# A graph diffusion with a routed feed-forward layer on one core: the last source tile stacked in the first step too, built blocks moved by 128 bytes, and early adds on VectorE

## The chip, the core and the metric

The program runs on one core of one Trainium2 chip. Its engines appear in the profile as PE (TensorE, matrix products into PSUM; PEld are its weight loads), DVE (VectorE), ACT (ScalarE), POOL (GpSimd) and SP (SyncE, here an issuer of DMA transfers). The metric is device time in microseconds (us); lower is better. "Profiled execution" means the one execution that the hardware profiler recorded; its own time is longer than its span by what lies around the first and the last instruction.

## The reference, cut to what matters

There are 3125 nodes with 256 features and 103,125 directed edges (50,000 in both directions, plus loops). The values at the edges' sources are summed at their destinations, divided by the degree, and this is repeated six times, each time divided by the step's number:

```python
def _spmm(h, src, dst, inv_deg):
    msg = h[src]
    agg = jax.ops.segment_sum(msg, dst, num_segments=h.shape[0])
    return agg * inv_deg[:, None]
...
out = h
term = h
for i in range(1, k + 1):                 # k = 6, gamma = 0
    term = (_spmm(term, src, dst, inv_deg) + gamma * term) / float(i)
    out = out + term
```

Around it: `h` is silu of a projection of the normalised input; the result is projected once more and added to the input. Then a router picks two of eight experts for each node, and their weighted outputs are added.

## The kernel before

Nodes are cut into 25 tiles of 128 rows (`NT = 25`, `P = 128`); the last has 53 rows only (`LAST`), less than half (`HP = 64`). The output projection is applied ahead of the diffusion, so that the terms have 256 columns (`D`) all the way.

**Terms in two parts.** A term is kept as two fp32r numbers, the rounded value and the rest, side by side: `t0` and `t1` are `[128, 25, 512]`. `split` (L350) makes both: a cast into the first 256 columns and a subtraction into the last 256. `t0` holds the terms of even steps, `t1` those of odd ones. Both begin at an address that is 480 modulo 512 bytes in each partition.

**Blocks.** For each destination tile j there is a block `blk` of 128 x 3200 numbers: for each source tile i a 128 x 128 piece that counts the edges from a source row to a destination row. `build_tile(j)` (L628) builds it in two halves: VectorE makes one-hot matrices (`left`, L638, and five `right`, L647), TensorE multiplies them in 40 small bf16 products (`pa`, L658), and ScalarE copies four results into the block (L662). The buffers of a half (pool `hot`) and the block's own (pool `blocks`, at 352 modulo 512 bytes) are double. At the end SP stores the block to DRAM (`adj[j]`). The last source tile has its real rows in the lower 64 partitions; in DRAM both halves of its piece hold the same numbers:

```python
full = (NT - 1) * P
nc.sync.dma_start(adj[j][:, :full], blk[:, :full].bitcast(F32))          # L666
for p in (0, HP):
    nc.sync.dma_start(adj[j][p:p + HP, full:], blk[:HP, full:].bitcast(F32))   # L668
```

**First step.** For each j, block j + 1 is built first, and then 25 products `pd` (L703), each 128 x 512, add up block j times `t0`. `finish` (L671) follows: ScalarE scales the columns of the rests (`low`, L675), VectorE forms `term` (L677) and writes both parts of it to `t1`. Engines run their instructions in the order in which a scheduler put them when the program was built.

**Steps two to six** (L1006 on). The block is loaded from `adj[j]` (L1008; pool `blocks2`, four buffers, at 480 modulo 512 bytes), in order on SP's queue, where the stores of the first step stand too. Here the last source tile is *stacked*: since only 64 of its partitions are needed, the upper 64 hold the term's parts crosswise (L681 to L683), and as both halves of the block's piece are equal, one 256-column product adds value and rest at once. It is multiplied second to last. `finish` adds the new term to the sum `acc` (L687) from the second step on.

**Early adds.** The projected input and the first step's term are added to `acc` later, in the second and the third step, by `add_late` (L689): three adds for a tile in the second step (with the bias), two in the third, on GpSimd. They read a tile of the buffer that `finish` writes anew in the same round.

**After the sixth step** come the lists of the router, the experts (L954, L963) and the weighted sums; the change does not touch them.

Of the kernel before, what the change touches and what calls it, by code (L numbers as in the profile page):

```python
# [10 lines left out]
F32 = mybir.dt.float32  # L11
# [9 lines left out]
P = 128  # L21
# [2 lines left out]
NT = 25  # L24
LAST = N - (NT - 1) * P
HP = P // 2
NE = 103125
NCH = (NE + P - 1) // P
G = 12
# [237 lines left out]
def tile_gnn_then_moe(  # L267
# [82 lines left out]
    def split(dst, v):  # L350
        nc.vector.tensor_copy(dst[:, :D], v)
        nc.vector.tensor_sub(dst[:, D:], v, dst[:, :D].bitcast(F32))

    lane = keys.tile([P, NH, CK, HALF], F16, name="lane")
# [180 lines left out]
                                  pk.rearrange("p k (h w) -> p k h w", w=HALF))  # L537
    before.close()
    hot = build.enter_context(tc.tile_pool(name="hot", bufs=2, reuse_waits="tile"))
    blocks = build.enter_context(tc.tile_pool(name="blocks", bufs=2, reuse_waits="tile"))  # L540
    ps_a = build.enter_context(tc.tile_pool(name="ps_a", bufs=2, space=bass.MemoryType.PSUM,
                                            reuse_waits="tile"))
# [33 lines left out]
    for t in range(0, NT, 2):  # L576
        n = min(2, NT - t)
        xt = proj.tile([P, 2, 2 * P], F32, name="xt")
        nc.scalar.copy(xt[:, :, :n * P], pt[:, :, :n * P])
        if t + 2 < NT:  # L580
            pt = normed(t + 2)
        ph = ps_o.tile([P, 2, 2 * P], F32, name="ph")
        ht = proj.tile([P, 2, 2 * P], F32, name="ht")
        for c in range(2):
            for k in range(2):
                nc.tensor.matmul(ph[:, c, :n * P], w_in_sb[:, k, c * P:(c + 1) * P], xt[:, k, :n * P],
                                 start=(k == 0), stop=(k == 1))
            nc.scalar.activation(ht[:, c, :n * P], ph[:, c, :n * P], AF.Silu,
                                 bias=b_in_pm[:, c:c + 1], scale=1.0)
        pm = ps_o.tile([P, 2, D], F32, name="pm")  # L590
        for q in range(n):
            for c in range(2):
                nc.tensor.matmul(pm[:, q, :], ht[:, c, q * P:(q + 1) * P], w_out_sb[:, c, :],
                                 start=(c == 0), stop=(c == 1))
        nc.vector.tensor_copy(t0[:, t:t + n, :D], pm[:, :n, :])
        nc.vector.tensor_sub(t0[:, t:t + n, D:], pm[:, :n, :], t0[:, t:t + n, :D].bitcast(F32))
    intro.close()
    ps_1 = build.enter_context(tc.tile_pool(name="ps_1", bufs=2, space=bass.MemoryType.PSUM,
                                            reuse_waits="tile"))
# [28 lines left out]
    def build_tile(j):  # L628
        blk = blocks.tile([P, NT * P], F32R, name="blk")
        by_dst = blk.rearrange("p (i q) -> p q i", q=P)  # L630
        for h in (2 * j, 2 * j + 1):
            if h * HALF * W >= N:
                half = blk.rearrange("p (i q) -> p i q", q=P)
                nc.vector.tensor_copy(half[:, :, HP:], half[:, :, :HP].bitcast(F32))
                continue
            left = hot.tile([P, CK, HALF // 2, P, 2], BF16, name="left")
            nl = CK * HALF // 2
            nc.vector.tensor_tensor(  # L638
                left.rearrange("p k a l u -> p (k a) l u"),
                steps[:, None, :P, :].to_broadcast([P, nl, P, 2]),  # L640
                lane[:, h, :, :].rearrange("p k (a u) -> p (k a) u", u=2)[:, :, None, :]
                .to_broadcast([P, nl, P, 2]), op=ALU.is_equal)
            right = []
            for k, (a, b) in enumerate(SPAN):
                m = (b - a) * NT
                r = hot.tile([P, HALF // 2, m, 2], BF16, name=f"right{k}")
                nc.vector.tensor_tensor(  # L647
                    r, steps[:, None, :m, :].to_broadcast([P, HALF // 2, m, 2]),
                    place[:, h, k, :].rearrange("p (a u) -> p a u", u=2)[:, :, None, :]
                    .to_broadcast([P, HALF // 2, m, 2]), op=ALU.is_equal)  # L650
                right.append(r)
            for a in range(HALF // 2):

                n = 2 * h + a
                pa = (ps_b if j > 1 and n % 3 == 2 else ps_a).tile([P, 2, 512], F32, name="pa")
                for u in range(2):
                    for k, (lo, hi) in enumerate(SPAN):
                        nc.tensor.matmul(pa[:, u, lo * NT:hi * NT], left[:, k, a, :, u],  # L658
                                         right[k][:, a, :, u], start=(k == 0), stop=(k == CK - 1),
                                         skip_group_check=True)  # L660
                q = ((h % 2) * HALF + 2 * a) * W
                nc.scalar.copy(  # L662
                    by_dst[:, q:q + 2 * W, :].rearrange("p (u q) i -> p u q i", u=2),
                    pa[:, :, :W * NT].rearrange("p u (q i) -> p u q i", i=NT))
        full = (NT - 1) * P
        nc.sync.dma_start(adj[j][:, :full], blk[:, :full].bitcast(F32))  # L666
        for p in (0, HP):
            nc.sync.dma_start(adj[j][p:p + HP, full:], blk[:HP, full:].bitcast(F32))  # L668
        return blk

    def finish(j, pd, step, new):  # L671
# [2 lines left out]
        low = work.tile([P, D], F32, name="low")  # L674
        nc.scalar.activation(low, pd[:, D:], AF.Copy, scale=inv)  # L675
        term = work.tile([P, D], F32, name="term")
        nc.vector.scalar_tensor_tensor(term, pd[:, :D], inv, low, op0=ALU.mult, op1=ALU.add)  # L677
        if new is not None and j < NT - 1:
            split(new[:, j, :], term)
        elif new is not None:  # L680
            nc.vector.tensor_copy(new[:HP, j, :D], term[:HP])  # L681
            nc.vector.tensor_copy(new[HP:, j, D:], term[HP:])
            nc.vector.tensor_sub(new[HP:, j, :D], term[HP:], new[HP:, j, D:].bitcast(F32))  # L683
            if step == 1:
                nc.vector.tensor_sub(new[:HP, j, D:], term[:HP], new[:HP, j, :D].bitcast(F32))
        if step > 1:
            nc.vector.tensor_add(acc[:, j, :], acc[:, j, :], term)  # L687

    def add_late(j, t, bias):  # L689

        term = early.tile([P, D], F32, name="early")
        part = t[:, j, :].bitcast(F32)
        nc.gpsimd.tensor_add(term, part[:, :D], part[:, D:])  # L693
        if bias:
            nc.gpsimd.tensor_add(term, term, b_out_sb)
        nc.gpsimd.tensor_add(acc[:, j, :], acc[:, j, :], term)

    blk = build_tile(0)
    for j in range(NT):
        ahead = build_tile(j + 1) if j + 1 < NT else None  # L700
        pd = ps_1.tile([P, 2 * D], F32, name="pd")
        for i in range(NT):
            nc.tensor.matmul(pd, blk[:, i * P:(i + 1) * P], t0[:, i, :],  # L703
                             start=(i == 0), stop=(i == NT - 1))
        finish(j, pd, 1, t1)
        if 8 <= j < 8 + len(tests):
            check_spans(j - 8)
        elif j == 8 + len(tests):
# [291 lines left out]
    for step in range(2, STEPS + 1):  # L1000
# [5 lines left out]
        for j in range(NT):  # L1006
            blk = blocks.tile([P, NT * P], F32R, name="blk")
            nc.sync.dma_start(blk.bitcast(F32), adj[j])  # L1008
            if step < 4:
                add_late(j, new, step == 2)  # L1010
            pd = ps_d.tile([P, 2 * D], F32, name="pd")
            for i in [*range(NT - 2), NT - 1, NT - 2]:
                n = D if i == NT - 1 else 2 * D
                nc.tensor.matmul(pd[:, :n], blk[:, i * P:(i + 1) * P], old[:, i, :n],  # L1014
                                 start=(i == 0), stop=(i == NT - 2), skip_group_check=True)
            finish(j, pd, step, new if step < STEPS else None)
            if step == STEPS:
                route(j)
    lists_end()
# [83 lines left out]
```

## Time and profile before

| What | us |
|---|---|
| median of four runs (1339.10 to 1341.39) | 1340.15 |
| profiled execution, its own time | 1344.07 |
| its span, first to last instruction | 1342.30 |
| first product of the first step (L703) begins | 96.32 |
| last product of the first step begins | 327.3 |
| second step's first product (L1014) begins | 330.81 |
| last product of the sixth step begins | 1057.4 |
| VectorE busy, whole span | 582.0 |
| GpSimd busy, whole span | 208.6 |

The rows of the last two lines are sums over the span. The others are places in it: the first step takes from 96 to 328, the five following steps from 331 to 1058, the experts and sums the rest. A matmul's row in the trace begins when it starts; its end is modelled, and the next matmul starts before it. So the distance between two starts is what a product costs in a row of products, not the length in the row.

### The profile page before, as it was taken

The page shows a single profiled execution, that of the slowest core. Times are in us where ns is not written, and L with a number is a line of the kernel's source. Part 1 is how long each engine was busy: PE and PEld are TensorE (multiplying, and loading weights), DVE is VectorE, ACT ScalarE, POOL GpSimd, SP SyncE. Part 2 cuts the span into 40 slices and gives each one's busy share as a digit, 9 for nine tenths or more (in the row PEclk, how much of TensorE's full clock was granted, in tenths as well). Part 3 has the DMA queues.
Part 4 walks back from the last instruction along what each step waited for, and adds up shares of the span by engine and source line. Part 5 has one row for each costly group of instructions (what it writes and reads, how often), then busy time and mean ns, then how long its engine had stood idle before and what let it go on. Part 6 is the DMA issues. An engine that isn't in the chain of part 4 may idle for free. (4 is left out here: it accounts for less than half of the span.)

```text
span 1342.3 us, 16667 instructions
## 1 busy us (share of the span) xinstructions
PE 1233.9 (92%) x6181; PEld 1017.6 (76%) x6181; DVE 582.0 (43%) x1436; ACT 347.2 (26%) x534; POOL 208.6 (16%) x264
## 2 busy tenths in 40 slices
PE   4999999999999999999999999999999559999940
PEld 2778888887888888888888888887777448888830
DVE  6769999994432222222222222245555412222116
ACT  5656667673000000000000000012222212222210
POOL 2000000007942200000000000001233222222210
PEclk9999999999999999999999999999999869999985
DMA  6014343436888888888888888887888277677728
GB/s 196 1 73 173 148 196 147 197 147 266 326 293 295 294 296 294 293 294 294 294 293 296 293 295 294 296 300 257 283 283 282 73 218 222 215 249 228 236 87 270
DMA packets 86246, 318.47 MB, mean 237 GB/s; under 512 B 12254, under 2 KB 56237, under 8 KB 66953
## 3 DMA queue, kind: packets, MB, share of 16 engines
q1 hardware_dynamic: 74550, 297.14, 62.5%
q0 software_dynamic: 5280, 14.54, 3.1%
q10 hardware_dynamic: 6322, 5.60, 1.3%
q8 instruction: 52, 0.85, 0.2%
q14 instruction: 42, 0.34, 0.1%
HBM read 256.44 MB, written 60.81 MB: 236 GB/s over the span
## 5 line engine op out<-in xcount | busy, mean ns | idle before, releaser
L1014 PE MATMUL pd<-t,blk 128*128 128x512 f32 (+1 forms) x3125 | 714.4, 388 | 3.1 <-DMA blk<-adj 3.1
L1014 PEld LDWEIGHTS pd<-t,blk 128*128 128x128 f32 x3125 | 576.2, 189 | 120.8 <-issue 3.5
L677 DVE SCALAR_TENSOR_TENSOR term<-pd,inv_deg,low 128x256 f32<-128x256 f32 x150 | 72.4, 483 | 454.5 <-ACT low L675 454.4
L675 ACT ACTIVATE low<-pd,inv_deg 128x256 f32<-128x256 f32 x150 | 71.1, 474 | 650.5 <-PE pd L1014 578.5
L703 PE MATMUL pd<-t,blk 128*128 128x512 f32 x625 | 151.1, 398 | 0.0
L662 ACT CAST blk<-pa 128x800 fp32r<-128x800 f32 x98 | 146.7, 1652 | 12.2 <-PE pa L658 12.2
L703 PEld LDWEIGHTS pd<-t,blk 128*128 128x128 f32 x625 | 115.9, 188 | 25.3
L647 DVE TENSOR_TENSOR right<-steps,place 128x800 bf16<-128x800 f16 (+3 forms) x245 | 127.9, 577 | 3.3 <-PE pa L658 3.3
L954 PE MATMUL ph<-xt,w_sb 128*128 128x256 f32 x432 | 100.6, 387 | 2.4 <-DMA w_sb<-in_w_dram 1.3
L658 PE MATMUL pa<-right,left 128*128 128x200 bf16 (+3 forms) x980 | 98.9, 254 | 0.9 <-ACT blk L662 0.7
L963 PE MATMUL py<-w_sb,ht 128*128 128x256 f32 x432 | 97.7, 379 | 0.0
L658 PEld LDWEIGHTS <-left 128*128 128x128 bf16 x980 | 83.4, 97 | 16.4 <-DVE right L647 5.7
L954 PEld LDWEIGHTS ph<-xt,w_sb 128*128 128x128 f32 x432 | 83.5, 194 | 14.7 <-DVE xt L946 3.1
L956 ACT ACTIVATE ht<-ph,b_sb 128x256 f32<-128x256 f32 x108 | 51.0, 473 | 144.6 <-PE ph L954 144.6
L963 PEld LDWEIGHTS py<-w_sb,ht 128*128 128x128 f32 x432 | 80.1, 190 | 9.9
L693 POOL TENSOR_TENSOR early<-t 128x256 f32<-128x256 f32 x50 | 37.7, 763 | 266.6 <-DVE right L647 264.7
L967 POOL DMA_INDIRECT ys<-y,xr x54 | 51.8, 958 | 161.6 <-DVE y L966 141.6
L638 DVE TENSOR_TENSOR left<-steps,lane 128x2560 bf16<-128x2560 f16 x49 | 72.7, 1483 | 1.1 <-PE pa L658 1.1
L946 DVE COPY xt<-px 128x512 f32<-128x512 f32 x27 | 18.7, 691 | 109.5 <-PE px L943 91.4
L848 POOL DMA_INDIRECT xs<-xg,to x50 | 48.8, 977 | 106.8 <-DVE m L787 38.8
L746 POOL IOTA lane_f<- 128x1 f32 x1 | 0.1, 137 | 415.3 <-PE pd L1014 415.3
L687 DVE TENSOR_TENSOR acc<-acc,term 128x256 f32<-128x256 f32 x125 | 55.6, 445 | 0.9
(198 smaller groups left out, 636.5 us busy)
## 6 DMA issues: line engine op xcount, KB each, us to landing
blk<-adj SPq DMA_DIRECT2D x125, 1600.0 KB, 6.9
adj<-blk SPq DMA_DIRECT2D x25, 1536.0 KB, 5.2
w_sb<-in_w_dram SPq DMA_DIRECT2D x54, 512.0 KB, 5.4
xr<-xs SPq DMA_DIRECT2D x27, 257.0 KB, 3.0
got<-ys SPq DMA_DIRECT2D x8, 640.0 KB, 7.0
b_sb<-in_b_dram SPq DMA_DIRECT2D x27, 128.0 KB, 5.1
out_dram<-acc ACTq DMA_DIRECT2D x24, 128.0 KB, 5.0
xs<-pad SPq DMA_DIRECT2D x9, 257.0 KB, 5.2
```

What stands on the lines that cost most here:

```text
L638: nc.vector.tensor_tensor(left.rearrange("p k a l u -> p (k a) l u"), steps[:, None, :P, :].to_broadcast([P, nl, P, 2]), lane[:, h, :, :]. ...
L647: nc.vector.tensor_tensor(r, steps[:, None, :m, :].to_broadcast([P, HALF // 2, m, 2]), place[:, h, k, :].rearrange("p (a u) -> p a u", u=2 ...
L658: nc.tensor.matmul(pa[:, u, lo * NT:hi * NT], left[:, k, a, :, u], right[k][:, a, :, u], start=(k == 0), stop=(k == CK - 1), skip_group_ch ...
L662: nc.scalar.copy(by_dst[:, q:q + 2 * W, :].rearrange("p (u q) i -> p u q i", u=2), pa[:, :, :W * NT].rearrange("p u (q i) -> p u q i", i=NT))
L675: nc.scalar.activation(low, pd[:, D:], AF.Copy, scale=inv)
L677: nc.vector.scalar_tensor_tensor(term, pd[:, :D], inv, low, op0=ALU.mult, op1=ALU.add)
L687: nc.vector.tensor_add(acc[:, j, :], acc[:, j, :], term)
L703: nc.tensor.matmul(pd, blk[:, i * P:(i + 1) * P], t0[:, i, :], start=(i == 0), stop=(i == NT - 1))
L954: nc.tensor.matmul(ph, got[1][:, k, q * P:(q + 1) * P], xt[:, k, :], start=(k == 0), stop=(k == 1))
L963: nc.tensor.matmul(py, ht[:, q, h * P:(h + 1) * P], got[2][:, q, :], start=(q == 0), stop=(q == HT - 1))
L967: nc.gpsimd.indirect_dma_start(ys_at[2 * i + h], bass.IndirectOffsetOnAxis(ap=got[0][:, h, D:].bitcast(U32), axis=0), y, None)
L1014: nc.tensor.matmul(pd[:, :n], blk[:, i * P:(i + 1) * P], old[:, i, :n], start=(i == 0), stop=(i == NT - 2), skip_group_check=True)
```

## The change

`ORDER` names the order of source tiles that steps two to six already use, with the last tile second to last. The first step now uses it and the 256-column product for the last tile. For that, `t0`'s last tile is written crosswise as well: the four operations that `finish` had are a function, `stack`, used for both. The block in SBUF needs its upper half filled before the product, so SP first copies the lower half of the last piece onto the upper one, within SBUF, and then stores the block in one transfer (the store waits for the copy). A tile of 128 bytes a partition, never used, stands between the pools `hot` and `blocks`; the built blocks now begin at 480 modulo 512 bytes. `add_late` runs on VectorE, and its first add is held until the last operation of the previous tile's `finish` in the instruction order.

```diff
+ORDER = (*range(NT - 2), NT - 1, NT - 2)
...
+    def stack(new, v, again):
+
+        j = NT - 1
+        nc.vector.tensor_copy(new[:HP, j, :D], v[:HP])
+        nc.vector.tensor_copy(new[HP:, j, D:], v[HP:])
+        nc.vector.tensor_sub(new[HP:, j, :D], v[HP:], new[HP:, j, D:].bitcast(F32))
+        if again:
+            nc.vector.tensor_sub(new[:HP, j, D:], v[:HP], new[:HP, j, :D].bitcast(F32))
...
     hot = build.enter_context(tc.tile_pool(name="hot", bufs=2, reuse_waits="tile"))
+
+    build.enter_context(tc.tile_pool(name="gap", bufs=1)).tile([P, 128], mybir.dt.uint8, name="gap")
     blocks = build.enter_context(tc.tile_pool(name="blocks", bufs=2, reuse_waits="tile"))
...
-        nc.vector.tensor_copy(t0[:, t:t + n, :D], pm[:, :n, :])
-        nc.vector.tensor_sub(t0[:, t:t + n, D:], pm[:, :n, :], t0[:, t:t + n, :D].bitcast(F32))
+        if t < NT - 1:
+            nc.vector.tensor_copy(t0[:, t:t + n, :D], pm[:, :n, :])
+            nc.vector.tensor_sub(t0[:, t:t + n, D:], pm[:, :n, :], t0[:, t:t + n, :D].bitcast(F32))
+        else:
+            stack(t0, pm[:, 0, :], True)
...
         full = (NT - 1) * P
-        nc.sync.dma_start(adj[j][:, :full], blk[:, :full].bitcast(F32))
-        for p in (0, HP):
-            nc.sync.dma_start(adj[j][p:p + HP, full:], blk[:HP, full:].bitcast(F32))
+        nc.sync.dma_start(blk[HP:, full:].bitcast(F32), blk[:HP, full:].bitcast(F32))
+        nc.sync.dma_start(adj[j], blk.bitcast(F32))
         return blk
...
-        nc.vector.scalar_tensor_tensor(term, pd[:, :D], inv, low, op0=ALU.mult, op1=ALU.add)
+        put = nc.vector.scalar_tensor_tensor(term, pd[:, :D], inv, low, op0=ALU.mult, op1=ALU.add)
...
-            nc.vector.tensor_copy(new[:HP, j, :D], term[:HP])
-            nc.vector.tensor_copy(new[HP:, j, D:], term[HP:])
-            nc.vector.tensor_sub(new[HP:, j, :D], term[HP:], new[HP:, j, D:].bitcast(F32))
-            if step == 1:
-                nc.vector.tensor_sub(new[:HP, j, D:], term[:HP], new[:HP, j, :D].bitcast(F32))
+            stack(new, term, step == 1)
         if step > 1:
-            nc.vector.tensor_add(acc[:, j, :], acc[:, j, :], term)
+            put = nc.vector.tensor_add(acc[:, j, :], acc[:, j, :], term)
+        return put
 
     def add_late(j, t, bias):
...
-        nc.gpsimd.tensor_add(term, part[:, :D], part[:, D:])
+        nc.vector.tensor_add(term, part[:, :D], part[:, D:])
         if bias:
-            nc.gpsimd.tensor_add(term, term, b_out_sb)
-        nc.gpsimd.tensor_add(acc[:, j, :], acc[:, j, :], term)
+            nc.vector.tensor_add(term, term, b_out_sb)
+        nc.vector.tensor_add(acc[:, j, :], acc[:, j, :], term)
...
-        for i in range(NT):
-            nc.tensor.matmul(pd, blk[:, i * P:(i + 1) * P], t0[:, i, :],
-                             start=(i == 0), stop=(i == NT - 1))
-        finish(j, pd, 1, t1)
+        for i in ORDER:
+            n = D if i == NT - 1 else 2 * D
+            nc.tensor.matmul(pd[:, :n], blk[:, i * P:(i + 1) * P], t0[:, i, :n],
+                             start=(i == 0), stop=(i == NT - 2), skip_group_check=True)
+        last = finish(j, pd, 1, t1)
...
             if step < 4:
-                add_late(j, new, step == 2)
+                with tc.issue_after(last.ins):
+                    add_late(j, new, step == 2)
...
-            for i in [*range(NT - 2), NT - 1, NT - 2]:
+            for i in ORDER:
...
-            finish(j, pd, step, new if step < STEPS else None)
+            last = finish(j, pd, step, new if step < STEPS else None)
```

Line numbers with L are those of the kernel before. In the changed kernel the first step's product is L715, that of steps two to six L1027, the copy L681, the store L682 and the reload L1020.

## The prediction

> **What bounds the kernel now.** I read the page first (busy shares, slices), then the timeline of three tiles of the first step, then the timeline where the first step hands over to the second, then the windows. The page:
>
> ```profile
> PE 1233.9 (92%) x6181; PEld 1017.6 (76%) x6181; DVE 582.0 (43%) x1436; ACT 347.2 (26%) x534; POOL 208.6 (16%) x264
> PEclk9999999999999999999999999999999869999985
> ```
>
> TensorE has work nearly everywhere; the two thin slices, the router's end and the sums, are not touched. So each edit is priced by what it does to TensorE in its own stage. One tile of the first step, from the timeline (start, length, engine, line; brackets: idle before and who ended it):
>
> ```profile
> 188.84 3.72 PEld L658 LDWEIGHTS <-left 128*128 128x128 bf16 x40 [0.28 <-DVE right L647]
> 188.84 3.91 PE L658 MATMUL pa<-right,left 128*128 128x200 bf16 x40
> 189.55 0.48 DVE L677 SCALAR_TENSOR_TENSOR term<-pd,inv_deg,low 128x256 f32<-128x256 f32 x1 [0.62 <-ACT low L675]
> 192.57 6.06 PE L703 MATMUL pd<-t,blk 128*128 128x512 f32 x25
> 196.02 2.56 DVE L647 TENSOR_TENSOR right<-steps,place 128x800 bf16<-128x800 f16 x5
> 196.04 0.33 SPq L666 DMA_DIRECT2D adj<-blk  x1
> 196.41 1.81 SPq L668 DMA_DIRECT2D adj<-blk  x2
> 198.47 3.89 PE L658 MATMUL pa<-right,left 128*128 128x200 bf16 x40
> ```
>
> Building a block (L658) and multiplying by it (L703) alternate without a hole: a period of 198.47 - 188.84 = 9.63 us, of which the 25 products take 198.47 - 192.57 = 5.90. VectorE is nearly as full (one idle stretch of 0.62 per tile), so it is the next bound, 0.6 us away. The hand-over to the second step:
>
> ```profile
> 315.86 11.87 PE L703 MATMUL pd<-t,blk 128*128 128x512 f32 x50
> 318.28 1.02 DVE L634 CAST blk<-blk 128x1600 fp32r<-128x1600 f32 x1 [1.87 <-ACT blk L662]
> 319.34 0.33 SPq L666 DMA_DIRECT2D adj<-blk  x1
> 319.71 1.81 SPq L668 DMA_DIRECT2D adj<-blk  x2
> 321.63 23.82 SPq L1008 DMA_DIRECT2D blk<-adj  x6
> 330.81 15.44 PE L1014 MATMUL pd<-t,blk 128*128 128x512 f32 x55 [3.08 <-DMA blk<-adj]
> ```
>
> TensorE waits 3.08 us there for the first reload, not for arithmetic. The windows of that place and of ten tiles of the second step (us; PE, PEld, DVE, ACT, POOL busy; clock; DMA share; GB/s):
>
> ```profile
> 331.00:337.00 6.00, 6.00 (x15) 4.65 (x16) 0.69 (x1) 0.00 (x0) 6.00 (x9) 0.50 0.99 399
> 389.58:445.38 55.80, 55.80 (x252) 46.21 (x251) 14.46 (x40) 4.74 (x10) 15.88 (x20) 1.00 0.82 294
> ```
>
> After the wait TensorE runs at half clock; later it is saturated, 5.58 us a tile, VectorE busy a quarter.
>
> **The change part by part.**
>
> *Stacking the last source tile (first step).* One product in 25 shrinks from 512 to 256 columns. The second step already has that form. In its starts, read one by one, the next matmul begins 113 ns after the 256-wide one. In the first step the intervals are 315 ns after the build, then 228 to 242 with a mean of 232.3. So a tile loses 232 - 113 = 119 ns: 5.90 becomes 5.78.
>
> *Moving the built blocks by 128 bytes.* Blocks and terms then begin alike modulo 512 bytes, as in the steps after, where t1 or t0 is read and the intervals settle at 227 ns after about four matmuls. The last first-step tile, which follows another without a build between and with ScalarE and VectorE nearly idle, still shows 228 to 242, so neither of them is the cause. PSUM banks and the transfers running beside it differ too, so the row does not prove the alignment. Bounds: nothing; 22 intervals at 227 instead of 232.3, 0.12 us a tile; and on the bad side all 22 at 241, the largest that recurs, 0.19 us lost. I take the 227, the row with the same addresses modulo 512. A tile is then 315 + 3 x 231 + 18 x 227 + 232 (before the new wait) + 113 + 239 = 5,678 ns: 0.22 us less than 5.90. The Trainium skill (TensorE: Matmul & The Clock Gate, "Step-by-step: what each phase is for") speaks against this part: TensorE reads weights and moving data through two independent ports, so loading the next weights takes nothing from the running matmul. By that the move would be worth nothing.
>
> *How many tiles count.* Everything up to the end of block 24's build: tiles 0 to 22, so 23. Tiles 23 and 24 only lengthen the wait for the reload. 23 x 0.22 = **-5.1 us** (bounds -5.5 with 227 from the first interval on, -2.8 without alignment, +1.6 with 241).
>
> *New wait in the product.* Product 24, at place 23, waits for the copy of its lower half onto the upper. The copy is issued where the store was (186.38 for the tile multiplied from 192.57), 11 us before that place: covered. Behind it on TensorE stands all that follows, so if the cover went, it would cost the whole lateness, 25 times. The release itself is the 232 instead of 227 above.
>
> *The store waits for the copy.* One 128-row store replaces one of 128 and two of 64 rows; SP holds it until the copy lands. Inside the step the buffer is wanted again by the cast 13 us after the store was issued (186.38 to 199.60) and the store's last packet ends 5.1 us after issue (191.46): covered. At the end it is not: block 24's copy takes the place at 319.34, its store follows, and the reload stands behind both on SP and on the same queue. The first store packet began 0.82 us after issue (320.16), a 64-row transfer's packets take some 0.15, and the reload's last packet was 0.45 before TensorE moved (330.33, 330.78). The copy so costs at least 0.82 + 0.15 + 0.45 = 1.4 us. The two small issues it replaces gave the reload no delay: it was issued at 321.63, but its first packet is at 324.28, when the store's end. Above, the quickest landing by row is 3.0 us (xr, 257 KB) with some 0.8 of data, so 2.2. Bounds 1.3 to 2.3, taken **+1.7**. The Trainium skill (SBUF — State Buffer, "The DMA setup-cost knee") gives about 2 us for any transfer, and by it this term is +2.0.
>
> *Clock.* The wait grows from 3.1 to about 3.1 + 1.7 + 0.4 (two shorter tiles) = 5.2 us. The half clock cost 339.36 - 330.81 - 5.58 = 2.97 us and goes on costing. If it falls as soon after the last matmul as now and lasts as long, 1.0 us of it slips into the longer wait; if two in five executions escape it today (the wait is short) and none will, 0.4 x 2.97 = 1.2 are added on average. No run here shows how often. Taken **0**.
>
> *First terms.* The last tile's split of t0 becomes four 64-row operations instead of two at 0.42 (L595 and L596 at 93.77 and 95.51): +0.8 us of VectorE near 94, where it is full. The changed order also puts the first tile's term ahead of the last two "right" of block 2, so TensorE's second half of that build wants a "right" at 104.3 that I find ready at about 104.5. **+0.3**, once (0 to 0.6); after that 0.37 us of slack a tile takes it back.
>
> *Adds on VectorE.* Fifty tiles of the second and third step get three or two adds at 0.445 (L687's mean): 1.3 us on top of 1.7 in a period of 5.58, placed after the previous tile's last operation. Cover: the running tile's product. At a step's start the stacked parts are written about 3.3 us after the last product (0.67 to the end of ScalarE's L675, 0.48 term, 0.45 add, four times 0.42) and wanted 23 x 0.227 = 5.2 us after. GpSimd loses 97 us that nothing waited for. **0** (loss 0 to 0.5; a gain is excluded because TensorE is saturated there).
>
> Sum: -5.1 + 1.7 + 0 + 0.3 + 0 = **-3.1 us**. The profiled execution took 1344.07 (span 1342.30 and 1.77 around it), so 1341.0 for one like it. It lies 3.9 above the median of the four runs, 1340.15; there the forecast is **1337.1**.
>
> **Rivals.**
> *Alignment does nothing*: -2.8 + 2.0 = -0.8, 1339.4. The next weights' load and the moving data then don't hinder each other, and the intervals stay at 232. For it: PSUM banks and DMA traffic also differ between the steps. Against: both intervals, 227 and 232, exceed the 216 of the experts' products at L954, so something in these products does yield. Chance 0.16. (It is what the rule of the Trainium skill's page TensorE: Matmul & The Clock Gate, quoted above, would give.)
> *The hand-over hides the copy* (the reload's packets need not wait for the store to drain, or the half clock shortens): -5.1 + 0.3 to -4.8 us, 1335.4. Against: the reload's first packet at 324.28 follows the store's last. Chance 0.08.
> *The moved blocks collide more*, slower than before: every product of the first step at 241, which is slower as soon as the interval passes about 235: +1.6 + 2.0 = +3.6, 1343.8. For it: the interval is plainly irregular there. Against: equal offsets give 227 in 2,400 products. Chance 0.10.
>
> **How the numbers follow.** 0.2% is 2.7 us, about what a measurement of this kernel can tell from no change. The forecast case has 0.66, and its own range is 1335.8 to 1338.6; 0.7 of it lies below 1337.45. Faster: 0.46 + 0.08 = 0.54; same: 0.20 + 0.16 = 0.36; slower 0.10. The range 1335.0 to 1340.7 takes in the first two rivals and leaves out the third and some tails.
>
> **What would show it.** The first step's period should be 9.40 to 9.42 us instead of 9.63; 9.51 means stacking alone; 9.7 collision. Starts within L715 should settle at 227. The wait before the first L1027 product should be near 5 us. The term of VectorE should still wait for ScalarE in each first-step tile (about 0.35 us); if it waits for nothing, VectorE has become the bound. I am wrong if the period stays at 9.63 or the steps two to five leave 5.58 us a tile.

## The result, and the profile after

| | before | after |
|---|---|---|
| median, us | 1340.64 (60 runs) | 1338.39 (40 runs) |
| range, us | 1338.20 to 1354.03 | 1336.24 to 1340.53 |
| profiled execution, its own time | 1344.07 | 1339.06 |
| its span | 1342.30 | 1337.20 |
| start of the first step's first product to start of its tile 23 | 219.54 | 214.55 |
| start of tile 23 to the second step's first product | 14.95 | 15.38 |
| start of tile 23 to the second step's third tile | 29.07 | 29.51 |
| a tile of steps two to five | 5.58 | 5.58 |

The ratio is 0.9981, with a 95% interval of 0.9975 to 0.9987: 2.5 us faster (1.7 to 3.4). The forecast was 1337.1 with a range of 1335.0 to 1340.7. The gain lies below the 2.7 us that the forecast called the limit of "no change", though the interval of the ratio leaves out 1.

The page of the changed kernel, its engines and two of its groups (busy us and mean ns, then idle time before and its releaser):

```profile
PE 1227.0 (92%) x6181; PEld 1016.2 (76%) x6181; DVE 620.1 (46%) x1563; ACT 347.0 (26%) x534; POOL 113.2 (8%) x139
L715 PE MATMUL pd<-t,blk 128*128 128x512 f32 x625 | 145.7, 389 | 0.0
```

GpSimd (POOL) lost 95.4 us of work and VectorE gained 38.1; the share of TensorE is the same 92%, so the page alone shows nothing of where the time went. One tile of the first step does, in the timeline (start, length, engine, line):

```profile
188.90 5.82 PE L715 MATMUL pd<-t,blk 128*128 128x512 f32 x25
192.34 0.47 SPq L681 DMA_DIRECT2D blk<-blk  x1
194.11 0.32 SPq L682 DMA_DIRECT2D adj<-blk  x1
194.56 3.90 PE L673 MATMUL pa<-right,left 128*128 128x200 bf16 x40
195.26 0.48 DVE L691 SCALAR_TENSOR_TENSOR term<-pd,inv_deg,low 128x256 f32<-128x256 f32 x1 [0.35 <-ACT low L689]
198.28 1.40 PE L715 MATMUL pd<-t,blk 128*128 128x512 f32 x5
```

The 25 products take 194.56 - 188.90 = 5.66 us instead of 5.90. The mean period over 21 tiles is 9.411 us instead of 9.628. VectorE still waits 0.35 us for ScalarE, so it did not become the bound. The hand-over to the second step:

```profile
309.34 11.43 PE L715 MATMUL pd<-t,blk 128*128 128x512 f32 x50
312.79 0.47 SPq L681 DMA_DIRECT2D blk<-blk  x1
314.53 0.33 SPq L682 DMA_DIRECT2D adj<-blk  x1
314.91 18.88 SPq L1020 DMA_DIRECT2D blk<-adj  x5
324.71 11.46 PE L1027 MATMUL pd<-t,blk 128*128 128x512 f32 x37 [3.94 <-DMA blk<-adj]
```

The store now stands 314.53 - 312.79 = 1.74 us behind the copy, and TensorE waits 3.94 us for the reload where it waited 3.08. The windows show the clock afterwards (TensorE, weight load, VectorE, ScalarE, GpSimd busy; granted clock; DMA share; GB/s):

```profile
325.00:330.00 5.00, 5.00 (x13) 3.84 (x13) 0.00 (x0) 0.00 (x0) 0.00 (x0) 0.50 1.00 424
```

So 5 us are won in 23 tiles, and some is given back at the hand-over. In this pair of profiles that is only 0.4 us, which would leave 4.5 us of gain, while the medians show 2.25. That difference is one question of the experiments; the others are whether each part earns what it was priced at, and whether moving the adds matters.

### The profile page after: what moved, and what is told of

Same layout as the page of the kernel before. It is cut to its first block, busy times and chain, and to the rows that moved or that the text cites. A ratio compares the mean times of both kernels' runs of the same rounds, so it can differ in the third digit from the quotient of the medians.

```text
span 1337.2 us, 16609 instructions
## 1 busy us (share of the span) xinstructions
PE 1227.0 (92%) x6181; PEld 1016.2 (76%) x6181; DVE 620.1 (46%) x1563; ACT 347.0 (26%) x534; POOL 113.2 (8%) x139
## 5 line engine op out<-in xcount | busy, mean ns | idle before, releaser
L1027 PE MATMUL pd<-t,blk 128*128 128x512 f32 (+1 forms) x3125 | 714.4, 388 | 3.9 <-DMA blk<-adj 3.9
L1027 PEld LDWEIGHTS pd<-t,blk 128*128 128x128 f32 x3125 | 576.2, 189 | 121.6 <-issue 4.2
L691 DVE SCALAR_TENSOR_TENSOR term<-pd,inv_deg,low 128x256 f32<-128x256 f32 x150 | 72.4, 483 | 409.7 <-ACT low L689 409.6
L715 PE MATMUL pd<-t,blk 128*128 128x512 f32 x625 | 145.7, 389 | 0.0
L715 PEld LDWEIGHTS pd<-t,blk 128*128 128x128 f32 x625 | 115.4, 188 | 23.1
L978 DVE TENSOR_TENSOR y<-py,b_sb 128x256 f32<-128x256 f32 x54 | 22.9, 425 | 70.6 <-PE py L975 70.6
L697 DVE TENSOR_TENSOR acc<-acc,term 128x256 f32<-128x256 f32 x125 | 52.4, 419 | 0.9
```

The lines of the kernel that those rows point to most:

```text
L691: put = nc.vector.scalar_tensor_tensor(term, pd[:, :D], inv, low, op0=ALU.mult, op1=ALU.add)
L697: put = nc.vector.tensor_add(acc[:, j, :], acc[:, j, :], term)
L715: nc.tensor.matmul(pd[:, :n], blk[:, i * P:(i + 1) * P], t0[:, i, :n], start=(i == 0), stop=(i == NT - 2), skip_group_check=True)
```

## The experiments

The twelve runs came in three groups, each on another chip: the kernel before had a median of 1361.43 us in the first, 1359.76 in the second and 1343.45 in the third. The two long ones come from the sixth step: in the profiles of those two chips TensorE pauses there three or four times for 2.5 to 4.1 us, and all but one of these pauses are followed by half clock (from the sixth step's start to its last product 184.9 us in the second group's profile of the kernel before, 165.8 in the third's, where neither shows). Why those chips pause there was not found. Times are therefore compared within a group, and stages of the first steps across groups.

**The stacking without the moved blocks.** The changed kernel without the unused 128 bytes; blocks begin at 352 modulo 512.

```diff
-    build.enter_context(tc.tile_pool(name="gap", bufs=1)).tile([P, 128], mybir.dt.uint8, name="gap")
```

> The changed kernel with the built blocks back at 352 modulo 512 bytes (the 128 unused bytes taken out), all else as changed. If the place modulo 512 sets the interval of the first step's products: starts 228 to 242 ns apart again, mean 232, period of a first-step tile 9.51 us (9.41 in the changed kernel), 23 tiles x 0.10 = 2.3 us slower than the changed kernel. If something else in the change made the intervals settle at 227 (the new wait at place 23, the 256-column product): period stays 9.41 and the time stays that of the changed kernel.

Measured: 1360.62 us, ratio 0.9992 (0.9981 to 1.0002), so not clearly below the kernel before; the changed kernel itself was not in this group. The period is 9.503 us and the intervals between starts are 228 to 241 ns again.

**The moved blocks without the stacking.** The kernel before with only the unused 128 bytes.

```diff
+    build.enter_context(tc.tile_pool(name="gap", bufs=1)).tile([P, 128], mybir.dt.uint8, name="gap")
```

> The kernel before with the 128 unused bytes alone. If the place modulo 512 sets the interval: products of the first step settle at 227, period 9.63 - 0.11 = 9.52 us, the wait at the hand-over stays near 3.1 us because stores and reload are as before, and the time falls by 23 x 0.11 = 2.5 us (1338.1 against 1340.6). If it needs the rest of the change: period 9.63, time as before.

Measured: 1358.89 us, ratio 0.9978 (0.9968 to 0.9988). The period is 9.520 us and the intervals settle at 227 ns. The two kernels' first-step products in the timeline, stacking alone and then moved blocks alone:

```profile
190.19 5.94 PE L714 MATMUL pd<-t,blk 128*128 128x512 f32 x25
195.97 3.77 PE L672 MATMUL pa<-right,left 128*128 128x200 bf16 x38
```

```profile
191.58 5.93 PE L704 MATMUL pd<-t,blk 128*128 128x512 f32 x25
197.35 2.35 PE L659 MATMUL pa<-right,left 128*128 128x200 bf16 x23
```

5.78 and 5.77 us from start to start, against 5.90 before and 5.66 with both. Each part earns 0.12 us and they add up. What follows: the place of the blocks is a cause of its own, and the rival "alignment does nothing" falls. The moved blocks alone gained 3.0 us (1.6 to 4.4), about as much as the whole change; they leave the hand-over as it was (the table further on).

**Blocks at another place.** An unused tile of 384 bytes in place of 128; blocks begin at 224 modulo 512, the terms at 480.

```diff
-    build.enter_context(tc.tile_pool(name="gap", bufs=1)).tile([P, 128], mybir.dt.uint8, name="gap")
+    build.enter_context(tc.tile_pool(name="gap", bufs=1)).tile([P, 384], mybir.dt.uint8, name="gap")
```

> The changed kernel with an unused tile of 384 bytes a partition in place of 128: the built blocks begin at 224 modulo 512 bytes, which is 256 away from the terms' 480. Theory: what counts is that weights and moving data begin alike modulo 512; then the intervals within the first step's products stay irregular as without the gap, 228 to 242, and the period is 9.50 us. Rival: they need only be alike modulo 256 bytes; then the intervals settle at 227 and the period is 9.41 to 9.42, as in the changed kernel. Second rival: only the first place (352) was bad; then 227 too, which this run alone would not tell from the rival before.

Measured, in a single execution: 1337.04 us, a period of 9.415 us, intervals settled at 227. So weights and moving data need not begin alike modulo 512 bytes, as the forecast put it. Either 256 is what counts or 352 was merely a bad place; this run does not tell these two apart.

**The adds back on GpSimd.** The changed kernel with `add_late` as it was before.

```diff
-        nc.vector.tensor_add(term, part[:, :D], part[:, D:])
+        nc.gpsimd.tensor_add(term, part[:, :D], part[:, D:])
...
-                with tc.issue_after(last.ins):
-                    add_late(j, new, step == 2)
+                add_late(j, new, step == 2)
```

> The changed kernel with the early adds back on GpSimd and not held back. My theory: they lie beside products either way, so steps two to five stay at 5.58 us a tile and the time is that of the changed kernel within 0.5 us. Rival: the adds on VectorE cost something that the one profile does not show (a part of the 2 us that are missing between the step's 5 us and the 2.25 us of the medians); then this kernel is 1 to 2 us faster than the changed one.

Measured: 1370.53 us, ratio 1.0039 (1.0015 to 1.0064), in two clusters: four runs at 1358.8 to 1360.1 and eight at 1370.4 to 1372.7. The first step's period is unchanged (9.416). The profiled execution is one of the long ones; its timeline:

```profile
334.09 1.43 POOL L707 TENSOR_TENSOR acc<-acc,early 128x256 f32<-128x256 f32 x2
335.61 22.83 DVE L352 CAST t<-term 128x256 fp32r<-128x256 f32 x1
358.37 0.41 DVE L697 TENSOR_TENSOR acc<-acc,term 128x256 f32<-128x256 f32 x1
360.09 8.17 PE L1026 MATMUL pd<-t,blk 128*128 128x512 f32 x23 [8.92 <-DVE term L691]
```

A cast that takes 0.29 us elsewhere stood for 22.83 us, while GpSimd ran its adds without a hole from 305 on. The first hole, of 78 ns, comes at 358.29, at the end of the second step's adds, and the cast ended at 358.44. TensorE, whose three PSUM buffers VectorE did not empty, then waited 8.92 us for the term. With this hand-over the early adds are therefore not free on GpSimd, although the forecast had it that nothing waits for them there. In the kernel before, whose adds run without a hole from 310 to 366, VectorE's cast and the sum's add went through, only slower (0.29 and 0.41 us elsewhere):

```profile
340.70 0.70 DVE L351 CAST t<-term 128x256 fp32r<-128x256 f32 x1
341.33 0.95 DVE L687 TENSOR_TENSOR acc<-acc,term 128x256 f32<-128x256 f32 x1
```

**The cast taken off VectorE.** The same kernel, with line 352 on ScalarE.

```diff
-        nc.vector.tensor_copy(dst[:, :D], v)
+        nc.scalar.copy(dst[:, :D], v)
```

> The variant with the early adds on GpSimd, in which VectorE's cast of a term once took 22.83 us and 8 of 12 executions were some 12 us longer; here that cast (line 352, the rounded half of every term) is done by ScalarE instead, and nothing else differs. Theory: VectorE's cast needs a moment in which GpSimd is not at SBUF, and 75 adds back to back leave none; with the cast gone from VectorE no operation stalls for more than 2 us and the long executions disappear: 1 to 5 us below the kernel before, all runs within 5 us of each other. Rival: it is the data (an add of GpSimd and the term's write touch the same buffer, and one waits for the other); then ScalarE's cast stalls in the same place, and executions some 12 us longer remain. Second rival: any VectorE operation is locked out, so that the subtraction behind the cast stalls instead; then the long executions remain too, with VectorE's subtraction in the trace in place of the cast.

Measured: 1368.27 us, ratio 1.0043 (1.0015 to 1.0072), all eight runs between 1363.98 and 1369.97. The theory, that the cast alone is shut out, falls; so does the first rival, since ScalarE's cast runs through:

```profile
335.56 0.41 ACT L352 CAST t<-term 128x256 fp32r<-128x256 f32 x1 [0.60 <-DVE term L691]
335.57 24.02 DVE L697 TENSOR_TENSOR acc<-acc,term 128x256 f32<-128x256 f32 x1
```

What stands still is whatever VectorE does next after the term, here the sum's add, for 24.02 us. That is the second rival, with the add in the subtraction's place. The term itself (L691), which reads PSUM, took its usual 0.48 us just before. The Trainium skill (SBUF — State Buffer, "Who interferes with whom") says that VectorE and GpSimd share a pair of SBUF ports as an exclusive lock, which VectorE needs for casts in its two-port modes and for operations with two SBUF inputs, and that the one that comes second blocks until the first instruction finishes. Which operations are shut out agrees with the traces. The duration does not: one add of GpSimd takes 0.72 us, and VectorE stood for 22.83 and 24.02, through more than thirty of them. The stop of 24.02 us, too, ended with the first hole of 78 ns in GpSimd's adds, 0.3 us after it began.

**The last store freed from the copy.** The changed kernel, with block 24 stored by the three transfers of before.

```diff
-        nc.sync.dma_start(adj[j], blk.bitcast(F32))
+        if j < NT - 1:
+            nc.sync.dma_start(adj[j], blk.bitcast(F32))
+        else:
+            nc.sync.dma_start(adj[j][:, :full], blk[:, :full].bitcast(F32))
+            for p in (0, HP):
+                nc.sync.dma_start(adj[j][p:p + HP, full:], blk[:HP, full:].bitcast(F32))
```

> The changed kernel, but the store of block 24 alone is made of the three transfers of before, which read only what ScalarE and VectorE wrote, so that it does not wait for the copy. In the changed kernel's profile the store is issued 1.74 us after the copy. If the hand-over is where the rest of the gain went: the store follows the copy by about 0.5 us, the wait before the second step's first product falls from 3.9 to about 2.5 us, and the time falls by 1.0 to 1.5 us, more where TensorE's clock then does not fall. If the missing 2 us are elsewhere: the wait falls, and the time by no more than 1.2 us.

Measured: 1356.59 us, ratio 0.9962 (0.9949 to 0.9976), or 5.2 us below the kernel before; the changed kernel was not in this group.

```profile
315.09 0.58 SPq L685 DMA_DIRECT2D adj<-blk  x1
325.99 4.38 PE L1032 MATMUL pd<-t,blk 128*128 128x512 f32 x12 [3.44 <-DMA blk<-adj]
```

The store goes out 0.5 us after the copy (314.58), as expected. The wait falls only to 3.44 us, not to 2.5 (3.83 from start to start), and the half clock lasts 3.4 us.

**Both kernels again, for the hand-over.** The kernel before was profiled twice more (1360.31 and 1340.52 us, each in its own group), the changed one once more and timed.

> The kernel before, unchanged, for a second profile beside the others of this group. Expected by every theory: a period of 9.62 to 9.63 us in the first step, intervals of 228 to 242 ns, 14.9 us from the start of the first step's tile 23 to the second step's first product. What is open is the half-clock stretch after the wait: if it is always 6.8 us long it can't explain why the changed kernel gained 2.25 us where its stages add up to 4 us; if it is 3.4 us in some executions, or begins at another place, one to two us can come and go there whatever the kernel.

> The changed kernel, unchanged, in the same group as its variants. Theory A: the stages decide (5.0 us won in 23 first-step tiles, 0.5 to 1 us lost at the hand-over), and the 2.25 us measured first were on the low side by chance; then 3.5 to 4.5 us below the kernel before. Theory B: about 1.5 us are lost at a place that the two profiles don't show, for instance a longer half-clock stretch in most executions; then 1.7 to 3 us below, as at first.

> The kernel before once more, for a third profile of its hand-over. In its first profile TensorE paused for 3.5 us there, start to start, and then ran at half clock for 6.8 us; in the second it paused for 2.6 us and did not drop. The changed kernel has paused for 4.3 us in both of its profiles and dropped for 6.8 us in both. Theory: a pause near 2.5 us is often too short to bring the clock down, one over 4 us always does, so the change lost on average a part of the 3 us that the half clock costs; expected here: a pause of 2.6 to 3.5 us, with or without the drop. Rival: the drop depends on nothing but the moment; then it will be missing in one of the changed kernel's profiles or variants with a long pause as well.

The changed kernel took 1356.79 us, ratio 0.9972 (0.9960 to 0.9985), or 3.8 us less (2.0 to 5.4). Its first step repeats (period 9.420). The third profile of the kernel before, hand-over and clock:

```profile
318.15 0.33 SPq L666 DMA_DIRECT2D adj<-blk  x1
320.44 21.35 SPq L1008 DMA_DIRECT2D blk<-adj  x6
329.45 5.83 PE L1014 MATMUL pd<-t,blk 128*128 128x512 f32 x25 [2.90 <-DMA blk<-adj]
```

```profile
330.00:335.00 5.00, 5.00 (x24) 4.12 (x22) 0.51 (x1) 0.00 (x0) 5.00 (x8) 1.00 0.96 351
```

The clock stays at 1.00: 24 products in 5 us, where the changed kernel did 13. All profiles in which SP issues the first reload (us; the pause is from the start of the last first-step product to the start of the next):

| kernel | pause | half clock for | tile 23 to second step | to its third tile |
|---|---|---|---|---|
| before | 3.48 | 6.8 | 14.95 | 29.07 |
| before, again | 2.62 | none | 14.10 | 26.61 |
| before, third | 3.30 | none | 14.77 | 26.60 |
| moved blocks alone | 2.76 | 3.4 | 14.00 | 26.69 |
| changed | 4.34 | 6.8 | 15.38 | 29.51 |
| changed, again | 4.31 | 6.8 | 15.35 | 29.49 |
| blocks at 224 | 4.35 | 3.4 | 15.39 | 28.04 |
| stacking alone | 4.09 | 3.4 | 15.32 | 28.20 |
| last store freed | 3.83 | 3.4 | 14.87 | 27.76 |
| copy at the last block alone (next experiment; adds on GpSimd) | 4.52 | 6.8 | 15.99 | 29.82 |
| adds back on GpSimd | 4.88 | 6.8 | 15.91 | 29.89 |
| cast taken off VectorE (adds on GpSimd) | 5.05 | 3.4 | 16.09 | 28.87 |

The first pair of profiles misled: the kernel before had the half clock in it, and in two other profiles it had not. In one of these two the second step also began 14.10 us after tile 23, not 14.9 as expected. From tile 23 to the third tile of the second step the three profiles of before take 27.43 us on average, the changed kernel 29.50 in two, 29.01 with the third that has the same hand-over (blocks at 224). That is 1.6 to 2.1 us lost. With 4.84 won up to tile 23 (means of 219.50 and 214.66), the stages give 2.8 to 3.3 us, inside both measured intervals.

By its time, 3.8 us less, the changed kernel lies where theory A put it, but the interval takes in theory B too. The profiles show a loss of the kind that theory B looked for, from the other side: the changed kernel's half clock is not longer, but the kernel before escapes it in two of three profiles. An escape saves less than the 2.97 us that the prediction gave the half clock: from the second step's first product to its third tile the kernel before takes 14.12 us with half clock, 12.51 and 11.83 without, because its second tile then waits up to 1.2 us for its own reload. With so few profiles the share of undisturbed hand-overs in the kernel before stays rough.

No profile with a pause over 3.4 us kept its clock; the Trainium skill (TensorE: Matmul & The Clock Gate, "HAM oscillation — how this bites in real kernels") gives about 3.4 us of idleness as the limit. The moved blocks alone fell to half clock after 2.76 us, so the traces agree only roughly. The kernel before kept its clock through 3.30 us, so the length of the pause alone does not decide.

**The copy at the last block alone.** The kernel before, with the copy and the waiting store for block 24 and no other part of the change.

```diff
+        if j == NT - 1:
+            nc.sync.dma_start(blk[HP:, full:].bitcast(F32), blk[:HP, full:].bitcast(F32))
+            nc.sync.dma_start(adj[j], blk.bitcast(F32))
+            return blk
```

> The kernel before with one edit: block 24, and it alone, is copied within SBUF and then stored in one transfer that waits for the copy, as in the changed kernel. No product is shorter and no block is moved, so this is the change's cost at the hand-over by itself. Theory: the reload's data come 0.9 to 1.7 us later, TensorE's pause grows from 2.6 to 3.5 us (before) to 4.2 to 4.9 us, and half clock follows for 6.8 us every time: 1 to 3 us slower than the kernel before, 23.5 to 24.5 us from the start of tile 23 to the start of the second step's tile 1 (before: 23.50 and 20.94 in two profiles). Rival: the hand-over is not where the missing gain is; then 0.4 us or less.

Measured: 1356.6 us, ratio 1.0056 (1.0020 to 1.0092), again in two clusters: four runs at 1343.8 to 1345.5, six at 1356.0 to 1359.1. The hand-over and VectorE behind it:

```profile
331.64 13.64 PE L1018 MATMUL pd<-t,blk 128*128 128x512 f32 x48 [4.12 <-DMA blk<-adj]
341.23 22.72 DVE L351 CAST t<-term 128x256 fp32r<-128x256 f32 x1
```

The pause is 4.52 us and half clock follows, as expected; the four short runs lie on average 1.2 us above the median of before. The second step begins 15.99 us after tile 23, where the three profiles of before have 14.61 on average: the copy by itself costs 1.4 us there. What was not expected is the cast that stands for 22.72 us. This kernel has neither stacking nor moved blocks, so the copy at the hand-over suffices to bring it on while the adds are on GpSimd, in six of ten runs if their times tell. Among the 127 runs of the unchanged kernel three stand 10 to 12 us above the next longest (1354.03, 1356.60 and 1375.08 in groups at 1341, 1343 and 1360). That looks like the same stop, but none of the three was profiled.

**The first reload issued by GpSimd.** The changed kernel; the second step's first reload no longer stands behind block 24's store.

```diff
-            nc.sync.dma_start(blk.bitcast(F32), adj[j])
+            (nc.gpsimd if step == 2 and j == 0 else nc.sync).dma_start(blk.bitcast(F32), adj[j])
```

> The changed kernel with one transfer moved: the second step's first reload is issued by GpSimd, which has nothing else to do there, instead of standing behind block 24's copy and store on SP's queue. It is free to start when block 24 is built (its buffer lies over the one-hot matrices), near 310 instead of 314.9, so its data should be in place by about 316 and the store near 321. Theory: the wait of 3.9 us before the second step's first product is the reload standing behind copy and store on SP, so it goes, and 3.5 to 4 us with it; with no pause TensorE also should not drop to half clock, which is worth up to 3 us more: 4 to 7 us below the changed kernel. Rival 1: the wait moves to the second tile's reload, which now stands behind a store that shares the engines with the first reload: it lands 5 us after the store, near 326, wanted at 326.3; if the two share badly it is late by 2 to 4 us and most of the gain goes: 0 to 2 us below. Rival 2: GpSimd writes the transfer's descriptors slowly or starts it no earlier: no gain.

Measured: 1352.19 us, ratio to the kernel before 0.9940 (0.9925 to 0.9956), 4.6 us below the changed kernel in the same group. Its timeline:

```profile
310.38 0.66 POOL L1020 DMA_DIRECT2D blk<-adj  x1 [266.14 <-PE pa L673]
318.33 0.33 SPq L682 DMA_DIRECT2D adj<-blk  x1
320.77 5.75 PE L1027 MATMUL pd<-t,blk 128*128 128x512 f32 x25
323.61 20.40 SPq L1020 DMA_DIRECT2D blk<-adj  x6
330.65 14.62 PE L1027 MATMUL pd<-t,blk 128*128 128x512 f32 x57 [4.13 <-DMA blk<-adj]
```

The second step begins without a pause, and then the second tile waits 4.13 us: rival 1, although the time gained is the theory's. Its reload waits for block 24's store, because its buffer lies over that block, and the store was held until 318.33 by a copy that shared the engines with the first reload. Of the 4.6 us only 1.1 are won at the hand-over (28.41 against 29.49 to the third tile); 0.5 lies ahead of the first product, and 2.7 are shorter pauses and less half clock (10.2 instead of 13.7 us) in the sixth step, 179.9 instead of 182.6 us, which the edit does not touch. That is one profile of each kernel; how the other runs divide is not known.

**Both edits of the hand-over together.** The first reload on GpSimd, and block 24's store freed from the copy; to the diff of the freed store comes:

```diff
-            nc.sync.dma_start(blk.bitcast(F32), adj[j])
+            (nc.gpsimd if step == 2 and j == 0 else nc.sync).dma_start(blk.bitcast(F32), adj[j])
```

> Two variants together: the second step's first reload is issued by GpSimd, and block 24 is stored by the three transfers that don't wait for the copy. With the first alone the pause went from the second step's first tile to its second: 4.13 us for a reload that had waited 4.9 us for block 24's store, since its buffer lies over that block; the store itself had been held until 318.33 by the copy, which shared the engines with the first reload. Theory: the store now goes out near 313.5 and is done near 320.5, the second reload lands near 326.5 where it is wanted at 326.3, and the pause shrinks to 0 to 1.5 us, too short to bring the clock down: 2.5 to 5 us below the variant with the first edit alone, 10 to 12.5 us below the kernel before. Rival: the store, the first reload and the copy share the engines, so that the copy lands after 320.4 and the last product of tile 24 waits for it, or the second reload is as late as it was: no gain over the first edit alone.

Measured: 1339.22 us in a group where the kernel before takes 1343.45, ratio 0.9964 (0.9950 to 0.9978).

```profile
323.28 20.58 SPq L1025 DMA_DIRECT2D blk<-adj  x6
330.48 14.87 PE L1032 MATMUL pd<-t,blk 128*128 128x512 f32 x58 [3.72 <-DMA blk<-adj]
```

The store went out at 313.71, but SP still waited 7.4 us for its end: it shares the engines with the first reload, so the second reload is issued at 323.28, hardly sooner than 323.61. The pause stays, as the rival said. Both versions are below the kernel before; the changed kernel was not in this group, and by the stages, up to the third tile, they are 1.1 and 1.5 us better than it.

## Why the prediction was right or wrong

**Faster by a little: right. The gain in the first step came out as worked out; the loss at the hand-over came out by luck, as errors cancelled.** Predicted -3.1 us, by stages -2.8 to -3.3, measured -2.5 (-1.7 to -3.4) and -3.8 (-2.0 to -5.4). By the prediction's own limit of 2.7 us the first of these is the case "same", which it gave 0.36.

- Stacking, 0.12 us a tile: 9.628 to 9.503, or 0.125. Right.
- Moved blocks, 0.10: 9.628 to 9.520, or 0.11. Right in size. The reason, equal places modulo 512 bytes, was too narrow: 224 does as well as 480.
- 23 tiles, -5.1: measured -4.84. Right, and so was the count: tiles 23 and 24 only lengthen the pause. The 25 products of a tile take 5.68 and 5.69 us on average in the two profiles, forecast 5.678.
- New wait at place 23: the next product comes 113 ns after the 256-wide one and nothing else shows. Covered, as said.
- The store behind the copy, +1.7: the path was right, and for the copy alone the size too. The store's issue moved by 1.74 us, and its first packet comes 2.55 us after the first issue instead of 0.82, so 1.7 later, as worked out. From there to the reload's first packet there are 4.4 us in the changed kernel, 4.1 in the kernel before. With the adds on GpSimd on both sides the second step begins 1.4 us later (15.99 after tile 23 with the copy at the last block alone, 14.61 before), inside the bounds of 1.3 to 2.3.
- But the changed kernel's second step begins at 15.37, only 0.8 later than before. The reload's data land 4.4 us after its first packet in both of its profiles, 5.24 to 6.05 us in the three of before; the prediction let the reload take as long as it did. With the same copy and store and the adds on GpSimd the reload takes 4.7 to 5.0 (the last three rows of the table), with the store in three transfers and the adds on VectorE 5.2 (last store freed). So both the moved adds and the single store go with a quicker reload. Why was not found.
- Clock, 0: mis-sized the other way. The text named it (executions that escape the half clock today and would not any more, 1.2 us) and then took nothing, because the one profile at hand showed the half clock. Of three profiles of before two escape; of the changed kernel none. Measured 0.8 to 1.3. This error and those of the store and the adds cancelled: the hand-over was forecast at +1.7 and lost 1.6 to 2.1.
- First terms, +0.3: not seen; the first period is 9.43 us in one profile and 9.44 in the other, the mean 9.41 and 9.42.
- Adds, 0: steps two to five keep 5.58 us a tile, so they cost nothing on VectorE. The step that failed is "a gain is excluded because TensorE is saturated there". At the hand-over TensorE waits, and there the second step begins 15.3 to 15.4 us after tile 23 with the adds on VectorE, 15.9 to 16.1 with them on GpSimd (seven profiles with copy and single store): some 0.6 us won. And with this change's own hand-over, adds left on GpSimd shut VectorE out in most runs and cost about 12 us. What the edit alone does to the kernel before was not run; by the times of its runs the long stop is rare there, so inside the change it is needed more than it would be without it.

Of the rivals, "alignment does nothing" was refuted by the moved blocks alone, "the blocks collide more" by the intervals of 227, and "the hand-over hides the copy" by the pause, which grew, though by less than forecast: near 5 us was expected, 3.94 and 3.91 came. The first of the three is what the rule of two independent read ports would give, which the prediction quotes. Here the measurement decides against it: moving the weights alone by 128 bytes changed the interval of the products.

## What to carry to other kernels

A product that is repeated hundreds of times should be read start by start: an irregular interval, here 228 to 242 ns instead of 227, can come from nothing but the place of the operands in SBUF, and an unused strip shows it. A saving inside a saturated loop is partly given back where the hand-over at its end grows, here 1.6 to 2.1 us of 4.84, and one profile of a place where the clock sometimes drops says little, so profile it a few times before pricing it. Work that is "free" on GpSimd can stop VectorE for more than 20 us while its instructions follow each other without a hole, in some executions and not in others.

## What the runs showed of the hardware that was not expected

- VectorE stood still for 22.83, 24.02 and 22.72 us in one instruction while GpSimd ran adds of 0.72 us back to back. In these three profiles VectorE had been idle for 9.78, 8.69 and 9.18 us before; in the kernel before, with the same adds, without a hole either, and no such stop, 8.43, 4.69 and 5.37. Each stop ended within 0.3 us of the first hole of 78 ns in GpSimd's adds. What decides whether it sets in was not found.
- The place of the weights alone, 352 against 480 or 224 modulo 512 bytes, changes the interval of 512-column products from a mean of 232.3 to a settled 227 ns.
- Half clock comes in stretches of 3.4 or 6.8 us at the hand-over, and the same kernel has it in one execution and not in the next, after pauses that differ by 0.2 us (3.48 and 3.30).
- A copy of 32 KB within SBUF holds the transfer that waits for it by 1.74 us; when a 1.6 MB reload shares the engines, by 5.4 (issue 312.95, store 318.33).
- The same reload of 1.6 MB took between 4.4 and 6.05 us from its first to its last packet, quickest behind a store of one transfer with the early adds on VectorE, slowest behind three transfers with the adds on GpSimd.
